# Attention of a macaron block: projections from seven block products, two steps at a time

## The chip, the cores and the metric

The kernel runs on one core of a Trainium2 chip. The metric is the device time of one launch in microseconds. The engines of the core work side by side and synchronise through semaphores: TensorE (in the profile PE for matmuls, PEld for weight loads), VectorE (DVE), ScalarE (ACT), GpSimd (POOL) and SyncE (SP, which here only issues DMAs).

## The reference

A sequence of 2048 tokens with 1024 features passes three parts, each with a residual sum: a feed-forward network (FFN) with weights of plus and minus one, an attention over blocks of 128 tokens behind a convolution of three taps, and the FFN again. All data are f32. Cut to what matters here:

```python
x = x + 0.5 * ffn(layernorm(x))
# attention
c = conv3(layernorm(x), conv_w) + conv_b            # 1024 -> 768 features
q, k, v = split(c, 3)                               # 256 features each, blocks of 128 tokens
qh = einsum('btd,dhe->bthe', q, wq) + bq            # 16 heads of 64
kh = einsum('btd,dhe->bthe', k, wk) + bk
vh = einsum('btd,dhe->bthe', v, wv) + bv
s = einsum('bqhe,bkhe->bhqk', qh / 8, kh)           # causal inside the block
p = softmax(where(causal, s, -1e9))
o = einsum('bhqk,bkhe->bqhe', p, vh)
o = einsum('bqhe,hed->bqd', o, wo) + bo             # 1024 -> 256
x = x + o @ proj_w + proj_b                         # 256 -> 1024
# second FFN
x = x + 0.5 * ffn(layernorm(x))
```

## The kernel before

`P` is 128, `NB` 512, `WC` 2 (256 features in two halves of 128 partitions), `NHP` 8 (16 heads in pairs of two), `NG` 4 groups of 512 tokens with `BPG` 4 blocks each. The kernel runs in order: first FFN, convolution, attention, second FFN. The convolution is done by six transformed tokens at a time. Its outputs leave one word (128 of the 768 features) at a time, first the two words of v, then q, then k (`WORDER`, line 494), each from VectorE (`outputs`, line 613) by SP into a DRAM buffer `qkv_dram`.

The attention's weights `wv_sb`, `wq_sb`, `wk_sb` are loaded during the convolution (line 807), and the first group's words are loaded back as each is stored (`load_qkv`, line 775).

Attention goes through 32 steps, one for each group and head pair (lines 844 and following). Each step has five stages, and a loop (line 1010) starts stage n of step i - n in the order 0, 1, 3, 2, 4:

- `stage_qkv` (846): two matmuls of 512 columns for q and two for k, one for each half of the 256 features, add up in a PSUM bank each; VectorE adds the bias on the way out (892, 894) into the tiles `qk`. At every fourth step (and for the first step both halves at once) the values of four head pairs are computed: for each of four blocks two matmuls of 512 columns, copied out by ScalarE or VectorE (875, 877). The same stage loads the next group's words, the residual rows (`xr`, 857), adds `proj_b` to them on POOL (860), and in group 2 loads the second FFN's weights and takes their signs on ScalarE (853).
- `stage_softmax` (898): for the two heads and four blocks of a step eight score matmuls of 64 rows; ScalarE copies them to SBUF (914), POOL masks (916), VectorE takes the maximum (926), ScalarE the four exponentials of a tile with their sums (929), VectorE normalises (936, 937).
- `stage_transpose` (940): eight transposes on TensorE, one tile copied back by ScalarE (948), one by VectorE (950).
- `stage_values` (953): eight matmuls of 64 output rows, bias by VectorE (967, tile `oT`).
- `stage_wo` (970): two matmuls of 512 columns per step, summed over the eight steps of a group in two banks `acc`; at the end ScalarE adds the bias (985, tile `o2T`).

`stage_proj` (988) follows once for each group: sixteen matmuls of 512 columns, whose banks VectorE adds to the residual rows (1002), which SP stores (1005). Behind the last step, pieces of the second FFN's beginning (`Ffn.fill`, 327: norms, transposes, gate, routing, scaling of its first tiles) are mixed in.

PSUM has four pools of two banks: `mm`, `acc`, `tr`, `sm` (line 72). In `before` q, k, values and output products use `mm`, scores `tr`, transposes and attention outputs `sm`.

A scheduler orders each engine's instructions when the program is built, by priority (program order, unless raised) and by its own estimate of when inputs are there; `pin` (102) keeps an instruction at its place in program order, and inside `tc.manual_schedule` the order written is kept. At run time each engine executes its own list in that order.

## Time and profile before

| what | us |
|---|---|
| median of three runs (968.71 to 968.81) | 968.72 |
| the profiled execution's own time | 967.74 |
| its span, first to last instruction | 965.6 |
| attention: first value product to the second FFN's first main product | 419.0 to 808.9 |
| the last key product to the same end | 766.0 to 808.9 |
| TensorE's granted clock | 0.999 of full speed |

The profile page shows one execution. A line of a group names the line of the kernel, engine, operation, output and inputs, their shape, the count, then the busy time in us and the mean duration of one in ns, and last the idle time of the engine in front of such instructions and what ended it. Matmuls are pipelined: the duration of one overlaps the next, so the time that a matmul costs is read from the distance of starts, or from busy time by count. A line of the order in time has the start, the length, engine, line, operation and count; what stands in brackets is the idle time before it and who ended it.

### The profile page before, as it was taken

The page shows a single profiled execution, that of the slowest core. Times are in us where ns is not written, and L with a number is a line of the kernel's source. Part 1 is how long each engine was busy: PE and PEld are TensorE (multiplying, and loading weights), DVE is VectorE, ACT ScalarE, POOL GpSimd, SP SyncE. Part 2 cuts the span into 40 slices and gives each one's busy share as a digit, 9 for nine tenths or more (in the row PEclk, how much of TensorE's full clock was granted, in tenths as well). Part 3 has the DMA queues.
Part 4 walks back from the last instruction along what each step waited for, and adds up shares of the span by engine and source line. Part 5 has one row for each costly group of instructions (what it writes and reads, how often), then busy time and mean ns, then how long its engine had stood idle before and what let it go on. Part 6 is the DMA issues. An engine that isn't in the chain of part 4 may idle for free.

```text
span 965.6 us, 13859 instructions
## 1 busy us (share of the span) xinstructions
PE 945.2 (98%) x5064; PEld 622.0 (64%) x5064; DVE 639.0 (66%) x1228; ACT 409.2 (42%) x1122; POOL 250.2 (26%) x319
## 2 busy tenths in 40 slices
PE   6999999999999999999999999999999999999997
PEld 4688878876666666655555455545554556878786
DVE  5798887799975566637656455646555665666654
ACT  5586665421111111125546254626452662444441
POOL 2555443410011011003313121212122312434341
PEclk9999999999999999999999999999999999999999
DMA  9776553698497675326030430044004216646331
GB/s 339 171 198 194 160 175 133 233 255 328 164 269 189 181 185 122 96 94 244 12 121 1 139 129 18 1 150 155 2 0 162 57 23 206 180 138 176 109 109 66
DMA packets 37522, 137.21 MB, mean 142 GB/s; under 512 B 4872, under 2 KB 5896, under 8 KB 35536
## 3 DMA queue, kind: packets, MB, share of 16 engines
q1 hardware_dynamic: 28336, 98.69, 28.3%
q0 software_dynamic: 8384, 29.63, 15.9%
q10 hardware_dynamic: 736, 8.02, 2.2%
q8 instruction: 40, 0.66, 0.3%
q14 instruction: 26, 0.21, 0.1%
HBM read 81.70 MB, written 37.85 MB: 124 GB/s over the span
## 4 chain that ended last, share of the span: by engine, by line
PE 54%; issue 30%; POOL 7%; DVE 4%; DMA 3%; ACT 3%; POOLq 0%; DVEq 0%; ACTq 0%
PE cv L542 22%; PE pm_f L309 20%; POOL xr L860 4%; PE tr_f L218 3%; PE pp L994 2%; POOL p L916 2%; DMA x<-in_x_dram 2%; PE lgp_f L226 2%; PE is_f L270 1%; PE tr L429 1%; DVE st_f L166 1%; DMA win<-xw 1%; ACT p L929 1%; PE po_f L293 0%; PE rt_f L258 0%
## 5 line engine op out<-in xcount | busy, mean ns | idle before, releaser
L309 PE MATMUL pm_f<-sw,y_f 128*128 128x512 f32 x1024 | 259.4, 404 | 0.6 <-ACT y_f L283 0.4
L309 PEld LDWEIGHTS pm_f<-sw,y_f 128*128 128x128 f32 x1024 | 187.3, 190 | 42.1 <-ACT y_f L283 0.8
L542 PE MATMUL cv<-v,u 128*128 128x342 f32 x576 | 166.0, 450 | 0.0
L542 PEld LDWEIGHTS cv<-v,u 128*128 128x128 f32 x576 | 109.0, 189 | 56.8
L916 POOL TENSOR_SCALAR_AFFINE_SELECT p<-p 128x512 f32<-128x512 f32 x64 | 39.7, 645 | 277.6 <-ACT p L914 230.1
L929 ACT ACTIVATE p<-p,anm 128x128 f32<-128x128 f32 x256 | 99.0, 389 | 7.1 <-DVE anm L926 7.1
L284 POOL TENSOR_TENSOR y_f<-xnT_f,y_f 128x512 fp32r<-128x512 f32 x63 | 79.8, 1281 | 65.2 <-ACT y_f L283 65.2
L321 DVE TENSOR_TENSOR pm_f<-pm_f,os_f 128x512 f32<-128x512 f32 x64 | 44.6, 697 | 69.4 <-PE pm_f L309 66.7
L559 ACT ACTIVATE m<-cv 128x342 f32<-128x342 f32 x42 | 19.2, 456 | 158.5 <-PE cv L542 157.1
L914 ACT COPY p<-sc 128x512 f32<-128x512 f32 x64 | 34.3, 587 | 104.0 <-PE sc L904 103.9
L926 DVE TENSOR_REDUCE anm<-p 128x4 f32<-128x512 f32 x64 | 40.9, 681 | 47.2 <-POOL p L916 47.2
L975 PE MATMUL acc<-oT,wo_sb 128*128 128x512 f32 x128 | 65.4, 595 | 0.0
L883 PE MATMUL pq<-qkv,wq_sb 128*128 128x512 f32 x128 | 60.6, 593 | 0.0
L883 PE MATMUL pq<-qkv,wk_sb 128*128 128x512 f32 x128 | 60.1, 592 | 0.0
L542 PE MATMUL cv<-v,g 128*128 128x342 f32 (+2 forms) x224 | 57.1, 415 | 0.9 <-DVE v L464 0.9
L994 PE MATMUL pp<-pw_sb,o2T 128*128 128x512 f32 x128 | 57.1, 599 | 0.4 <-DVE xr L1002 0.2
L867 PE MATMUL pv<-wv_sb,qkv 128*128 128x512 f32 x128 | 56.1, 592 | 0.0
L219 ACT COPY xnT_f<-tr_f 128x512 f32<-128x512 f32 x62 | 35.8, 587 | 46.1 <-PE tr_f L218 44.5
L530 DVE SCALAR_TENSOR_TENSOR u<-g,u 128x1024 f32<-128x1024 f32 x18 | 22.0, 1223 | 44.1 <-issue 41.4
L542 PEld LDWEIGHTS cv<-v,g 128*128 128x128 f32 x224 | 39.7, 190 | 17.6 <-DVE v L464 1.3
L929 ACT ACTIVATION_READ_ACCUMULATOR p<-p,anm 128x1 f32 x256 | 48.1, 188 | 0.0
L937 DVE TENSOR_TENSOR p<-p,asum 128x512 f32<-128x512 f32 x64 | 45.6, 712 | 2.2
(138 smaller groups left out, 1469.9 us busy)
## 6 DMA issues: line engine op xcount, KB each, us to landing
g<-in_conv_w_dram SPq DMA_DIRECT2D x28, 512.0 KB, 5.3
u<-in_conv_w_dram POOLq DMA_DIRECT2D x24, 512.0 KB, 6.4
x<-in_x_dram SPq DMA_DIRECT2D x16, 512.0 KB, 4.5
raw<-in_weight_t_dram SPq DMA_DIRECT2D x16, 512.0 KB, 6.6
x<-hbias POOLq DMA_DIRECT2D x16, 512.0 KB, 5.4
x<-x SPq DMA_DIRECT2D x16, 512.0 KB, 4.1
xr<-x SPq DMA_DIRECT2D x16, 512.0 KB, 6.6
x<-xr SPq DMA_DIRECT2D x16, 512.0 KB, 3.9
```

What stands on the lines that cost most here:

```text
L284: lows[h].tensor_tensor(yl, y, yh.bitcast(F32), ALU.subtract)
L309: ins = nc.tensor.matmul(pms[h], lhsT=y[:, n, c, :], rhs=self.sw[:, c, ts(h, NB)], start=(c == 0 and n == 0), stop=(c == DC - 1 and n == 1),)
L321: nc.vector.tensor_tensor(pms[h], pms[h], o, ALU.mult)
L542: nc.tensor.matmul(accs[w, k][:, lo:hi], lhsT=uk[:, c, :], rhs=V[k][:, c, lo:hi], start=(c == 0), stop=(c == DC - 1),)
L867: nc.tensor.matmul(pv, lhsT=qkvs[g][2][:, c, ts(b, P)], rhs=wv_sb[:, c, ts(half, NB)], start=(c == 0), stop=(c == WC - 1),)
L883: nc.tensor.matmul(pq, lhsT=w_sb[:, c, ts(hp, P)], rhs=qkvs[g][n][:, c, :], start=(c == 0), stop=(c == WC - 1),)
L916: nc.gpsimd.affine_select(out=p, in_=p, pattern=[[0, BPG], [-1, P]], compare_op=ALU.is_ge, fill=NEG_INF, base=0, channel_multiplier=1,)
L926: nc.vector.tensor_reduce(nmax, p, AX.X, ALU.max, negate=True)
L929: nc.scalar.activation(p[:, b, :], p[:, b, :], AF.Exp, bias=nmax[:, b : b + 1], accum_out=asum[:, b : b + 1],)
L937: nc.vector.tensor_tensor(p, p, asum.unsqueeze(2).broadcast_to([P, BPG, P]), ALU.mult)
L975: nc.tensor.matmul(accs[g][m], lhsT=wo_sb[:, hp, ts(m, P)], rhs=oT, start=(hp == 0), stop=(hp == NHP - 1),)
L994: nc.tensor.matmul(pp, lhsT=o2T[:, m, ts(b, P)], rhs=pw_sb[:, m, ts(h, NB)], start=(m == 0), stop=(m == WC - 1),)
```

## The change

Queries and keys of two steps (256 weight columns by 512 tokens, 256 features to sum over) are written as a product of two-by-two blocks and computed by seven block products instead of eight, after the scheme of Strassen in Winograd's form: sums of weight blocks (`row_sums`) and of token blocks (`column_sums`) are formed first, and each product's PSUM bank is read between products, so that one bank collects four products and the other three, each read giving one term of the four output blocks. Values are computed the same way, 256 tokens by 1024 weight columns at a time.

- In `seven`, a unit's products 0, 2, 4, 6 go to a bank of `mm` and 1, 3, 5 to one of `tr`; product 3 starts its bank anew, the others add. After each, `Leave` reads the bank: products 0, 2, 3, 6 by ScalarE (which writes the output half with bias and scale), products 1, 4, 5 by VectorE (which adds into it). Two units go in turn: q and k, or two pairs of token blocks for the values. The reads have raised priority.
- A block product of q or k has 256 moving columns, of v 512.
- Weight sums are formed once, on POOL; token sums for each group, for q on POOL, for k on VectorE, for v on POOL.
- The loop goes over 16 pairs of steps with TensorE's order written out: products of pair i, `wo` of pair i - 2, transposes of i - 1, scores of i, attention outputs of i - 1; at the first pair of a group (but the first) then the group's values, at the second pair the output product of the group before. Pieces of the second FFN stand between the stages of the last pairs.
- The four score banks of a pair, two of `mm` and two of `tr`, are copied by ScalarE before any exponential of the pair (`issue_after`).
- `proj_b` is added to the residual rows by an accumulating DMA that POOL issues, instead of a POOL operation. The residual rows are loaded one group later. The ring of rows has 6 buffers instead of 8, and four more are opened for the second FFN. The loads of the q, k and v words and of the FFN weights are placed anew.

```diff
+    def by_rows(w, extra):
+        w4 = w.rearrange("p c (i two e) -> p c i two e", two=2, e=P)
+        e3 = extra.rearrange("p n (i e) -> p n i e", e=P)
+        a11, a12, a21, a22 = (w4[:, j, :, i, :] for i in range(2) for j in range(2))
+        return {"a11": a11, "a12": a12, "s1": a21, "a22": a22, "s2": e3[:, 0], "s3": e3[:, 1], "s4": e3[:, 2]}
+
+    def row_sums(eng, parts):
+        a11, a12, a21, a22, s2, s3, s4 = (parts[n] for n in ("a11", "a12", "s1", "a22", "s2", "s3", "s4"))
+        eng.tensor_tensor(s3, a11, a21, ALU.subtract)
+        eng.tensor_tensor(a21, a21, a22, ALU.add)
+        eng.tensor_tensor(s2, a21, a11, ALU.subtract)
+        eng.tensor_tensor(s4, a12, s2, ALU.subtract)
...
+    def column_sums(eng, parts):
+        b11, b12, b21, b22, t2, t3, t4 = (parts[n] for n in ("b11", "t1", "b21", "b22", "t2", "t3", "t4"))
+        eng.tensor_tensor(t3, b22, b12, ALU.subtract)
+        eng.tensor_tensor(b12, b12, b11, ALU.subtract)
+        eng.tensor_tensor(t2, b22, b12, ALU.subtract)
+        eng.tensor_tensor(t4, b21, t2, ALU.subtract)
+
+    def seven(units):
+        for n, (sums, a, b) in enumerate((
+            (0, "a11", "b11"),
+            (1, "a12", "b21"),
+            (0, "s2", "t2"),
+            (1, "s1", "t1"),
+            (0, "s3", "t3"),
+            (1, "s4", "b22"),
+            (0, "a22", "t4"),
+        )):
+            for name, rows, cols, u, width, leave in units:
+                if n < 2:
+                    leave.sums[n] = bank(("mm", "tr")[n], [P, width], f"{name}_{n}")
+                nc.tensor.matmul(
+                    leave.sums[sums],
+                    lhsT=rows[a][:, u, :],
+                    rhs=cols[b],
+                    start=n in (0, 1, 3),
+                    stop=True,
+                    skip_group_check=True,
+                )
+                with tc.high_priority(offset=400):
+                    leave(n, leave.sums[sums])
+
+    class Leave:
+        def __init__(self, parts, put, more):
+            self.parts, self.put, self.more, self.sums = parts, put, more, {}
+
+        def __call__(self, n, acc):
+            i, first = {0: (0, 1), 1: (0, 0), 2: (1, 1), 3: (3, 1), 4: (3, 0), 5: (1, 0), 6: (2, 1)}[n]
+            (self.put if first else self.more)(self.parts[i], acc, i // 2)
...
-    rring = pool(b3, "rring", 8)
+    rring = pool(b3, "rring", 6)
...
+        tokens_of(0)
+        row_sums(nc.gpsimd, wk_parts)
+        token_sums(0, (nc.gpsimd, nc.vector))
...
+                def put(h, acc, j, n=n):
+                    bias = (sbq, bk_sb)[n][:, 2 * r + j : 2 * r + j + 1]
+                    nc.scalar.activation(h, acc, AF.Identity, bias=bias, scale=(QSCALE, 1.0)[n])
+
+                def more(h, acc, j, n=n):
+                    if n == 0:
+                        nc.vector.scalar_tensor_tensor(h, acc, QSCALE, h, ALU.mult, ALU.add)
+                    else:
+                        nc.vector.tensor_tensor(h, acc, h, ALU.add)
...
-                if n == 0:
-                    nc.vector.tensor_scalar(h, pq, bq_sb[:, hp : hp + 1], QSCALE, ALU.add, ALU.mult)
-                else:
-                    nc.vector.tensor_scalar(h, pq, bk_sb[:, hp : hp + 1], None, ALU.add)
...
+        def load_residual(g):
+            for t in range(g * BPG, (g + 1) * BPG):
+                rows[t] = rring.tile([P, D], F32, name=f"xr_{t}", tag="x")
+                pin(nc.sync.dma_start(out=rows[t], in_=x2[t]))
+                pin(nc.gpsimd.dma_start(out=rows[t], in_=proj_b.broadcast_to([P, D]), accum_op=ALU.add))
...
+        with tc.manual_schedule(engines={mybir.EngineType.PE}):
+            for i in range(LAST + 2):
+                g, r = divmod(i, NP)
+                if i == 0:
+                    stage_v(0)
+                if i < LAST:
+                    if r == 1 and g + 1 < NG:
+                        tokens_of(g + 1)
+                        vxs[g + 1] = values_of(g + 1)
+                    stage_qk(g, r)
+                    if r == NP - 1 and g + 1 < NG:
+                        token_sums(g + 1, (nc.gpsimd, nc.vector))
+                if r == 0 and g > 0:
+                    load_residual(g - 1)
+                for c in range(2):
+                    if i in SIGNS:
+                        signs(SIGNS[i] + c)
+                two(stage_wo, i - 2)
+                if i == LAST:
+                    some(4)
+                two(stage_transpose, i - 1, "sm", "tr")
+                if i < LAST:
+                    stage_scores(g, r)
+                two(stage_values, i - 1)
+                if i < LAST and r == 0 and i > 0:
+                    stage_v(g)
+                if i == LAST - 1:
...
+                    parts = ffn.fill()
+                    some(1)
+                if r == 1 and g > 0:
+                    stage_proj(g - 1)
+            some(len(parts))
```

## The prediction, made before the changed kernel was run

> **What bounds the kernel now.** I read the page's head first, then the busy times of two stretches, the TensorE groups with shapes kept apart, and the order of work over one step of attention.
>
> ```profile
> span 965.6 us, 13859 instructions
> ...
> PE 945.2 (98%) x5064; PEld 622.0 (64%) x5064; DVE 639.0 (66%) x1228; ACT 409.2 (42%) x1122; POOL 250.2 (26%) x319
> ```
>
> TensorE is busy for 98% of the span; no other engine passes 66%. In the stretches (PE, PEld, DVE, ACT, POOL; a count of instructions behind each) the first line is all of attention, the second its end, from the last key product to the first product of the last FFN:
>
> ```profile
> 419.00:808.90 389.90, 387.00 (x2020) 204.80 (x2018) 226.41 (x400) 187.91 (x666) 86.26 (x94) 1.00 0.26 87
> 766.00:808.90 42.90, 40.59 (x272) 22.97 (x271) 22.93 (x44) 21.04 (x61) 9.60 (x12) 1.00 0.39 96
> ```
>
> TensorE idles 2.9 us in attention, 2.3 of them at the end; VectorE stands at 58%, ScalarE at 48%. So TensorE work taken out of attention comes off the time, as long as no new wait appears. What is taken out has these prices:
>
> ```profile
> L542 PE MATMUL cv<-v,u 128*128 128x342 f32 x576 | 166.0, 450 | 0.0
> ...
> L883 PE MATMUL pq<-qkv,wq_sb 128*128 128x512 f32 x128 | 60.6, 593 | 0.0
> L883 PE MATMUL pq<-qkv,wk_sb 128*128 128x512 f32 x128 | 60.1, 592 | 0.0
> ...
> L867 PE MATMUL pv<-wv_sb,qkv 128*128 128x512 f32 x128 | 56.1, 592 | 0.0
> ...
> L542 PE MATMUL cv<-v,g 128*128 128x256 f32 x32 | 7.2, 378 | 0.0
> ```
>
> The count shows that an f32 matmul of the program is two instructions on the chip (q: 32 steps x 2 blocks = 64 matmuls, 128 instructions). "Mean" holds the pipeline's tail; the pace is what counts. The order of work in a step:
>
> ```profile
> 651.22 1.88 PE L883 MATMUL pq<-qkv,wq_sb 128*128 128x512 f32 x4
> 652.94 1.88 PE L883 MATMUL pq<-qkv,wk_sb 128*128 128x512 f32 x4
> ...
> 653.14 0.75 DVE L892 TENSOR_SCALAR qk<-pq,bq_sb 128x512 f32<-128x512 f32 x1 [1.89 <-PE pq L883]
> ...
> 660.68 0.40 ACT L929 ACTIVATE p<-p,anm 128x128 f32<-128x128 f32 x1
> ...
> 661.07 0.40 ACT L929 ACTIVATE p<-p,anm 128x128 f32<-128x128 f32 x1
> ...
> 779.99 1.04 ACT L219 COPY xnT_f<-tr_f 128x512 f32<-128x512 f32 x2
> ...
> 780.60 0.43 PE L226 MATMUL lgp_f<-xnT_f,gate_sb 128*32 128x128 f32 x8 [1.83 <-ACT xnT_f L219]
> ```
>
> Four q instructions take 652.94 - 651.22 = 1.72 us, 0.43 each. VectorE reads 0.20 us after the last one's pace ends (653.14). Exponentials follow one another every 0.39 us. TensorE starts about 0.03 us after the ScalarE result it needs (first of the two copies, 779.99 + 0.58).
>
> **The change, part by part.**
>
> *Products.* At 342 columns an instruction paces at 166.0/576 = 0.288 us. At 256 columns 32 took 7.2 us in two runs, each with one tail of 378 - 216 ns, so (7.2 - 0.32)/32 = 0.215; 0.288 x 256/342 gives 0.216 too. Queries and keys of two steps: before, 16 instructions x 0.43 = 6.88 us; after, 2 x 7 products x 2 instructions x 0.216 = 6.05. Gain 0.83 x 16 pairs = 13.3 us. Values: 128 x 0.43 = 55.0 becomes 112 x 0.43 = 48.2, gain 6.9. Together **-20.2 us**.
>
> The row of 256 columns (0.215 us) says that the narrower product is paced by its columns alone. The Trainium skill, TensorE: Matmul & The Clock Gate, "Why this matters for your kernels", speaks against narrowing: at least 85% of peak only with all dimensions at 512 or more. If that made 256 columns cost 0.216/0.85 = 0.254 us (an estimate from that page), q and k would lose 28 x 0.254 - 6.88 = 0.23 us a pair instead of gaining 0.83, 17 us worse in all, and the kernel would be slower. I go by the row: it is the same type, height and engine.
>
> *Waits between products.* Product n+2 of a unit adds into the bank that product n's reader must have left. With q and k in turn that is 4 x 0.43 = 1.72 us from start to start. The way round: product 0.43, wake 0.15 to 0.20 (a ScalarE copy of a value bank starts at 420.97, its four instructions at 419.10), read, 0.03 back. The ScalarE read (256 wide, bias by pointer) is not in the trace; o2T, the same form at 512, takes 676 ns, and copies of 128 and 512 columns 253 and 587, 0.87 ns a column, so 0.676 - 0.22 = 0.46. VectorE: 512 columns 0.69, 342 columns 0.52, so 0.43. The round is 1.07 to 1.10 us. The wait sits on the weight load, which starts some 0.2 us ahead of its matmul, so about 0.42 us is spare. An exponential under way holds ScalarE for at most 0.39, within it; a VectorE operation (reduce 0.68, oT 0.74) for up to 0.75, 0.3 over, in the two VectorE reads of a unit that a product waits for (the second and the fifth). Load of an ordinary pair without value or output work, 15.5 us of TensorE (6.05 + wo 3.44 + transposes 1.8 + scores 2.2 + values 2.1): ScalarE 4 copies 2.1, 16 exponentials 6.2, two pT copies 1.2, eight reads 3.0 = 12.5 (81%); VectorE reduces 2.6, reciprocals and products 3.5, oT 1.5, pT 1.4, six reads 2.6 = 11.6 (75%). The eight ScalarE reads are new there; the four VectorE bias adds of 0.75 go. Bounds for the stall of a pair: 0, and 1.54 us (one tile's four exponentials ahead of a read). I take 0.25, near the lower end since the usual hold fits the spare time: **+4 us** over 16 pairs.
>
> *Values into queries.* The first k product needs the bank of the second value unit, read by a copy of 0.58 us that starts 0.15 after the last value product, while q's first product covers 0.43: 0.3 us, four times: **+1.4 us** with the restart. Within the value products two units of 0.86 us give 3.4 us a round against 0.86 + 0.15 + 0.58 or 0.70: no stall. VectorE's 24 and ScalarE's 32 reads there lie under 12 us of TensorE.
>
> *Softmax of two steps together.* In nine rounds no value or output work follows the scores; the transposes come 2.1 + 6.05 + 3.44 = 11.6 us after the last score (the fourth tile's 1.3 later). ScalarE frees at +1.2 (two copies, 1.07), then 16 exponentials x 0.39 = 6.2 and six reads of the next pair 2.2 bring +9.6, reciprocal and product 0.9 more: 10.5 against 12.9. Nothing, with 2.4 us spare; if a wait ahead of the exponentials eats that, the transposes stall and with them everything behind in TensorE's written order.
>
> *Head of attention.* v of the first group is loaded long before. The store of the last k half is issued at 424.6 and its reload goes out at 428.45; today keys are first needed at 434.5, in the new order at 431.1 + 1.3 (419.05 + 12.0 of value products). Landing takes 2.6 to 4.7 us, so 431.1 to 433.2; then three VectorE sums (256 wide, 0.43) before the first t2 product at 433.2. Bounds 0 and 4; **+1.5 us**. On POOL the key weight sums (4 x 1.28, the row of 128x512 tensor operations) stand ahead of the query sums (4 x 0.65): 7.7 us from 424.6, done by 432.3. The query and value weight sums, 8 x 1.28 = 10.2 us, fall in the convolution, where POOL only issues DMAs with 2 to 8 us idle before each; SP holds the weight loads up to 10 us, which the taps, a word ahead, cover: 0, or up to 2 if not.
>
> *End of attention.* The last softmax now has four tiles: 10.5 - 2.2 (no reads) = 8.3 us, plus three normalisations of 1.24 and two copies of 0.58 on ScalarE = 13.2. Before it TensorE has values 2.1, wo 3.44 and some 3.4 of FFN pieces, whose own chains wait in the written order. That leaves 4.3 idle; then o2T before the output product about 1, and the first scaling, now behind the output product instead of ahead of it, about 1: 6.3 against the 2.3 idle today: **+4 us**, bounds 0 and 9.
>
> *The rest.* The POOL adds of proj_b (16 x 2.36 = 38 us) become accumulating DMAs (16 x 0.90 on POOL, 5.4 to land): neither is on the path, since the output product comes a whole round later; in the last group 12 us remain against 6.6 + 5.4, so 0, at most 2. Sums for later groups lie on POOL and VectorE in a round's last 9 us. Loads, stores and sign loads move within SP, whose DMA share is 0.26. SP blocked by a ring of six costs nothing while rows are read a round ahead.
>
> Sum: -20.2 + 4 + 1.4 + 1.5 + 4 = **-9.3 us**. The profiled execution took 967.74 (span 965.6 and 2.1 around it), so 958.4; the median of the runs shown, 968.72, lies 1.0 above it, which gives **959.4**.
>
> **Rivals.**
> - *Slower: the ScalarE queue.* It runs in written order. One tile's exponentials that still wait for their reduce stand ahead of a read: 4 x 0.39 = 1.54 us a pair, 24.6 instead of 4, so 980. It decides from 13.3/16 = 0.83 us a pair. For it: ScalarE at 81%, and 7.1 us idle before exponentials for that reason today. Against: reads are marked urgent, and all reduces end within about 4 us of the last score. The trace shows ScalarE starts only in order; the Trainium skill, same page, "Architectural detail", calls ScalarE and VectorE strict FIFO, which is what lets this rival live but gives no price.
> - *Softmax and end late.* 0.4 us in each of nine rounds and 6 at the end: 959.4 + 3.6 + 2 = 965. For it: 2.4 us spare only.
> - *All covered.* Only the 1.4 at the values stays: 968.7 - 20.2 + 1.4 = 950. For it: TensorE never waits today.
> - *No gain at 256 columns.* A 128-column weight load paces the product. L309 at 512 columns runs 16 in 3.86 us, 0.241 each: q and k gain 6.88 - 28 x 0.241 = 0.13 a pair, 2 instead of 13.3, so 970.6. Against: the 256-column row.
>
> **How the numbers follow.** Forecast 0.45 (955 to 964); late softmax 0.15; all covered 0.10; ScalarE queue 0.25 (972 to 988); weight loads 0.05. Faster by over 0.2% (2 us, about what a measurement of this kernel can tell from no change) is the first three, 0.70; within it 0.05; slower 0.25. The range leaves out the upper half of the queue's case and little below: 950 to 978; the likeliest case alone 955 to 964.
>
> **What would show it.** Right: products of 256 columns every 0.216 us; 8 and 6 reads a pair of about 0.46 and 0.43; idle time ahead of the q and k products below 0.4 us a pair; TensorE about 367 us busy in attention. Wrong: idle before these products put down to ScalarE reads (queue), idle before transposes (softmax), or a pace near 0.24.

## The result, and the profile after

The changed kernel takes 971.3 us (median of 20 runs) where the kernel before, on the same chip, takes 968.7 (20 runs). The ratio is 1.003 with an interval of 1.002 to 1.004: slightly slower. The forecast was 959.4, faster. The profiled execution of the changed kernel took 970.66; its span is 968.8, against 965.6 before, so 3.2 us have to be explained, and 9.3 us of gain that did not come.

The head of the page:

```profile
span 968.8 us, 14538 instructions
...
PE 930.2 (96%) x5240; PEld 662.9 (68%) x5240; DVE 649.8 (67%) x1289; ACT 464.6 (48%) x1262; POOL 268.4 (28%) x363
```

TensorE has 15.0 us less to do (945.2 to 930.2), yet idles 38.6 us instead of 20.4. The busy times of the same two stretches as before (all of attention; its end from the last key product to the first product of the second FFN):

```profile
421.76:806.09 384.33, 367.63 (x2169) 245.37 (x2167) 228.85 (x452) 240.57 (x800) 84.90 (x122) 0.98 0.39 115
756.49:806.09 49.60, 43.17 (x257) 24.67 (x255) 25.21 (x52) 22.18 (x67) 11.81 (x18) 0.93 0.86 237
```

TensorE is busy 367.6 us in attention, as forecast (about 367), though partly by luck: 11.3 us that the new order of work saves (below) were not in the forecast. It waits there 16.7 us instead of 2.9, 6.4 of them at the end, and its clock, 1.00 before, is down to 0.93 at the end. The groups of the new products and their reads:

```profile
L826 PE MATMUL pq<-x,wq_sb 128*128 128x256 f32 x96 | 31.2, 407 | 0.9 <-DMA x<-qkv 0.5 <-DVE qk L953 0.4
L949 ACT ACTIVATE qk<-pq,sbq 128x256 f32<-128x256 f32 x64 | 30.0, 469 | 45.8 <-PE pq L826 45.7
L955 DVE TENSOR_TENSOR qk<-pq,qk 128x256 f32<-128x256 f32 x48 | 20.2, 422 | 0.3
L826 PE MATMUL pq<-t,wq_sb 128*128 128x256 f32 x32 | 9.5, 379 | 0.0
```

The reads last 0.47 and 0.42 us (0.46 and 0.43 were assumed). The last line has the mean of a product without a wait, 379 ns, as the 378 of the convolution's 256 columns. So the products are not the surprise. The waits are, and they sit in few places. In the order of work at the head of attention (start, length, idle time before and who ended it):

```profile
434.42 0.67 PE L826 MATMUL pq<-x,wq_sb 128*128 128x256 f32 x2 [0.48 <-DMA x<-qkv]
436.07 0.67 PE L826 MATMUL pq<-x,wk_sb 128*128 128x256 f32 x2 [0.98 <-ACT qk L949]
...
438.92 0.67 PE L826 MATMUL pq<-x,wk_sb 128*128 128x256 f32 x2 [1.75 <-DMA x<-qkv]
...
441.06 1.19 PE L826 MATMUL pq<-t,wk_sums 128*128 128x256 f32 x2 [1.04 <-DVE t L809]
442.04 1.06 PE L826 MATMUL pq<-x,wq_sb 128*128 128x256 f32 x2
442.90 1.06 PE L826 MATMUL pq<-x,wk_sb 128*128 128x256 f32 x2
...
457.31 0.63 PE L1031 MATMUL pt<-ident,p 128*128 128x128 f32 x4 [0.58 <-DVE p L1024]
459.39 0.63 PE L1031 MATMUL pt<-ident,p 128*128 128x128 f32 x4 [1.46 <-DVE p L1024]
```

The first pair's queries and keys take 12.4 us (434.4 to 446.8) instead of 6.05: TensorE waits for keys on their way back from DRAM, then for VectorE's token sums, then runs at half pace (442.04 to 442.90: two instructions in 0.86 us instead of 0.43). The keys' second half is late because its reload stands behind the store of its own word. SP's issues in order of time (SPq), and its own wait:

```profile
428.49 0.32 SPq L640 DMA_DIRECT2D qkv<-y  x1
...
433.37 0.32 SPq L783 DMA_DIRECT2D x<-qkv  x1
```

```profile
SPq L783 <- DMA qkv<-y: 2.0, 1, 2.0
```

The first three halves go out at 428.9, 429.4 and 430.3, right behind the store of the last word; the fourth waits until that store has landed (4.9 us after its issue) and itself lands 5.4 us after its own, at 438.8. The first key half lands at 435.98, so the wait that ends at 436.07 is most likely for it, although the profile puts it down to a ScalarE read.

Pair 0's transposes wait for the softmax. ScalarE's order in time shows why it is long. The first and the last of pair 0's sixteen exponentials, with one of the reads of pair 1's products that stand among them:

```profile
450.85 0.44 ACT L1016 ACTIVATE p<-p,anm 128x128 f32<-128x128 f32 x1
...
451.67 0.47 ACT L949 ACTIVATE qk<-pq,sbq 128x256 f32<-128x256 f32 x1
...
459.36 0.40 ACT L1016 ACTIVATE p<-p,anm 128x128 f32<-128x128 f32 x1
```

They take 8.9 us; in the kernel with eight products everywhere (below), where VectorE reads q and k, 6.2:

```profile
444.26 0.40 ACT L996 ACTIVATE p<-p,anm 128x128 f32<-128x128 f32 x1
...
450.05 0.39 ACT L996 ACTIVATE p<-p,anm 128x128 f32<-128x128 f32 x1
```

The longest wait of the end, from the list of TensorE's waits:

```profile
PE acc L1061 <- DVE oT L1053: 4.2, 1, 4.2
```

and what stands ahead of that `oT` in VectorE's queue (its order in time):

```profile
764.13 1.27 DVE L166 BATCH_NORM_STATS2 st_f<-xf 128x6 f32<-128x512 f32 x2
...
766.20 1.87 DVE L1012 TENSOR_REDUCE anm<-p 128x4 f32<-128x512 f32 x3 [0.54 <-POOL p L1002]
768.48 0.69 DVE L1012 TENSOR_REDUCE anm<-p 128x4 f32<-128x512 f32 x1 [0.41 <-POOL p L1002]
...
769.17 0.72 DVE L1053 TENSOR_SCALAR oT<-ao,bv_sb 128x512 f32<-128x512 f32 x1
```

The attention outputs of pair 14 end at 765.7; their bias on VectorE comes at 769.17, behind the FFN's norm sums and the last softmax's four maxima, two of which wait for POOL.

For the experiments the span is cut at four points of TensorE's order: first value product, first output weight product of group 0 (`acc`), end of the last key product, first main product of the second FFN. The pieces are called head, middle, end, and behind. Within the changed order of work each stretch holds the same work in every kernel, unless the text says otherwise (the row of before holds it mixed differently: its end has about 2.1 us less of work):

| kernel | first value product at | head | middle | end | behind | span |
|---|---|---|---|---|---|---|
| before | 419.1 | 40.6 | 306.5 | 42.8 | 156.7 | 965.6 |
| changed | 421.8 | 51.8 | 283.0 | 49.6 | 162.7 | 968.8 |
| eight products everywhere | 420.3 | 43.1 | 294.3 | 52.4 | 160.5 | 970.7 |

Each row is one profiled execution. In the profiles of kernels whose head is written like the changed one's it lies between 49.1 and 53.3 us.

### The profile page after: what moved, and what is told of

It is laid out like the page before. It is cut to its first block, busy times and chain, and to the rows that moved or that the text cites. A ratio compares the mean times of both kernels' runs of the same rounds, so it can differ in the third digit from the quotient of the medians.

```text
span 968.8 us, 14538 instructions
## 1 busy us (share of the span) xinstructions
PE 930.2 (96%) x5240; PEld 662.9 (68%) x5240; DVE 649.8 (67%) x1289; ACT 464.6 (48%) x1262; POOL 268.4 (28%) x363
## 4 chain that ended last, share of the span: by engine, by line
PE 45%; ACT 4%; DVE 2%; issue 1%; POOL 1%; POOLq 0%; ACTq 0%; DVEq 0%
PE pm_f L309 12%; PE pq L826 7%; PE pp L1086 6%; PE acc L1061 5%; PE pv L826 4%; PE sc L989 3%; PE ao L1044 2%; PE pt L1031 2%; ACT p L1016 1%; PE tr_f L218 1%; PE lgp_f L226 1%; PE is_f L270 1%; ACT qk L949 1%; ACT p L998 0%; DVE t L807 0%
## 5 line engine op out<-in xcount | busy, mean ns | idle before, releaser
L309 PE MATMUL pm_f<-sw,y_f 128*128 128x512 f32 x1024 | 262.8, 407 | 0.7 <-ACT y_f L283 0.4
L1061 PE MATMUL acc<-oT,wo_sb 128*128 128x512 f32 x128 | 60.3, 616 | 4.2 <-DVE oT L1053 4.2
L949 ACT ACTIVATE qk<-pq,sbq 128x256 f32<-128x256 f32 x64 | 30.0, 469 | 45.8 <-PE pq L826 45.7
L1036 DVE COPY pT<-pt 128x512 f32<-128x512 f32 x32 | 22.1, 690 | 39.0 <-PE pt L1031 39.0
L295 ACT ACTIVATE os_f<-po_f 128x512 f32<-128x512 f32 x64 | 34.7, 595 | 28.1 <-PE is_f L270 17.9
L1061 PEld LDWEIGHTS acc<-oT,wo_sb 128*128 128x128 f32 x128 | 25.1, 198 | 30.0 <-issue 24.6
```

Of the source, the lines that this page charges most:

```text
L309: ins = nc.tensor.matmul(pms[h], lhsT=y[:, n, c, :], rhs=self.sw[:, c, ts(h, NB)], start=(c == 0 and n == 0), stop=(c == DC - 1 and n == 1),)
L949: nc.scalar.activation(h, acc, AF.Identity, bias=bias, scale=(QSCALE, 1.0)[n])
L1061: nc.tensor.matmul(accs[g][m], lhsT=wo_sb[:, hp, ts(m, P)], rhs=oT, start=(hp == 0), stop=(hp == NHP - 1),)
```

## The experiments

Each edit is cut to what matters; where a kernel builds on another one of this list, the edit is shown against that one. Each ratio is to the kernel before on the same chip.

### Four runs that split the loss

**The value sums moved on POOL.** The first group's value sums are pinned behind the last tap load of the convolution; nothing but POOL's order changes.

```diff
-        row_sums(nc.gpsimd, parts)
+        row_sums(nc.gpsimd, parts, pin if g == 0 else lambda ins: ins)
```

> The changed kernel with one edit: the four POOL sums over the first group's value words are queued behind the last tap DMA of the convolution; the order of every other engine stays. Theory (POOL's queue): in the changed kernel these sums wait 11.0 and 10.2 us on POOL for the value words to land, and the accumulating tap DMAs queued behind them go out 4 and 6 us later than before, which is what makes TensorE wait 2.8 us for u in the convolution. Expected: no wait of cv for u, the first value product some 3 us earlier (about 418.5 instead of 421.8), time about 968 against 971. Rival (the POOL weight sums slow VectorE through shared memory ports, so u is late anyway): cv still waits, time 971.

Measured: 968.4 us, ratio to before 1.000 (0.999 to 1.001); the first value product starts at 418.9 instead of 421.8, and TensorE no longer waits for taps in the convolution, as expected. In the changed kernel POOL's order in time is

```profile
301.55 0.72 POOL L795 TENSOR_TENSOR vs<-vx 128x256 f32<-128x256 f32 x1 [11.02 <-DMA vx<-qkv]
302.23 0.87 POOL L520 DMA_DIRECT2D u<-in_conv_w_dram  x1
...
329.70 0.72 POOL L796 TENSOR_TENSOR vx<-vx 128x256 f32<-128x256 f32 x1 [10.21 <-DMA vx<-qkv]
...
331.96 0.88 POOL L520 DMA_DIRECT2D u<-in_conv_w_dram  x1
```

and with the sums moved

```profile
294.58 0.87 POOL L520 DMA_DIRECT2D u<-in_conv_w_dram  x1 [3.66 <-DMA u<-in_conv_w_dram]
...
325.50 0.87 POOL L520 DMA_DIRECT2D u<-in_conv_w_dram  x1 [6.94 <-DMA u<-in_conv_w_dram]
```

A sum that waits 11 us for its operand holds the tap loads queued behind it; they go out 6 to 8 us later than with the sums moved, and TensorE then waits 2.8 us for taps. So 3 us of the loss are a queue position in the convolution, a place that the change does not seem to touch.

**Eight products.** The new order of stages with plain eight products of 512 columns, no sums.

```diff
-            seven(units)
+            for c in range(WC):
+                nc.tensor.matmul(pq, lhsT=w_sb[:, c, ts(hp, P)], rhs=xs[g][:, c, :], ...)
```

> The changed kernel with the old eight products in the new order: q, k and v by the plain two-block matmuls of 512 columns, biases on VectorE, no sums of weights or tokens; everything else (pairs, written order, DMAs of proj_b, the end) stays. Theory: the products cost 20.2 us more, but the waits between products (6 us), the waits of the first pair for sums (7 us) and the convolution's wait (3 us) go, and the pairs' order keeps its 0.6 us a pair: about 971 + 20 - 6 - 7 - 3 = 975, range 971 to 978, above the changed kernel. Rival (the waits between products ate the whole gain of 20 us): without them the time falls to 955 to 963.

Measured: 971.5 us, ratio 1.004 (1.003 to 1.006). The new order with all else that was moved along with it (loads, residual rows, signs) costs about 4 us against before, and the seven products bring about 1 us on top of it (1.9 by the two spans), which the intervals of the two ratios don't tell from nothing. By the table they win 11.3 us in the middle, and lose 8.7 at the head, 1.4 ahead of it and 2.2 behind; 2.8 more lie at the end, where these kernels have the same products, and their cause stays open. The number stands at the lower edge of the theory's; that the waits between products eat their gain is out. The order is not worse everywhere: what a pair does besides its queries and keys takes 9.16 us (3.43 + 1.84 + 1.99 + 1.90 for output weights, transposes, scores, attention outputs) in both new kernels, and 9.78 in two steps of before (8.33 from step to step, less 3.44 of products). Scores and attention outputs of one step of before, and of a pair in the changed kernel:

```profile
654.75 1.16 PE L904 MATMUL sc<-qk,qk 64*128 64x128 f32 x16
655.84 1.09 PE L958 MATMUL ao<-pT,vh 128*64 128x128 f32 x16
```

```profile
478.80 2.06 PE L989 MATMUL sc<-qk,qk 64*128 64x128 f32 x32
480.79 1.97 PE L1044 MATMUL ao<-pT,vh 128*64 128x128 f32 x32
```

From start to start 16 scores take 1.09 us, 32 of them 1.99. With fewer changes from one kind of matmul to another TensorE gains 0.6 us a pair, 9.8 in all, which the forecast did not have. The loss is ahead of attention and at its two ends.

**A filled array.** Matmuls into an unused bank stand where TensorE waits in pair 0 and ahead of the output weights of pair 14, to see whether the fallen clock costs the time.

```diff
+                if i == LAST:
+                    fill_array("mm", 10, wo_sb[:, 0, 0:P], wo_sb[:, 0, 0:HT])
                 two(stage_wo, i - 2)
```

> The changed kernel with useless matmuls of 256 columns (their results are read by nobody) in three places where TensorE waits: 9 in the first pair's products, 10 ahead of the last but one pair's output sums. Theory (granted clock): the waits there let the granted clock fall, and the products behind run at twice their duration (0.85 instead of 0.43 us; 6.1 instead of 3.4 us for the eight output-sum instructions at the end). With the array kept busy the clock stays at 1.00 there and 3 to 5 us come off: 966 to 968. Rival (the waits alone set the time, the low clock is hidden in them): 970 to 973, whatever the clock shows.

Measured: 972.3 us, ratio 1.005 (1.003 to 1.006), in the rival's range. At the end the filler takes 4.4 us in the place of the wait, and the output weights behind it run in 3.43 us instead of 6.1; but TensorE waits longer behind them, and the end shrinks only from 49.6 to 48.5. So half pace follows from the waits and costs some 2.7 us at the end, and with filler most of that is waited for elsewhere. For the head the run settles nothing: pair 0 takes 11.0 us instead of 12.4, but pair 1 waits 2.9 us for a VectorE read behind maxima whose masks stand, in this kernel, behind three value sums on POOL, and the head grows from 51.8 to 54.6.

**`oT` first.** The bias of the attention outputs gets raised priority on VectorE.

```diff
-            nc.vector.tensor_scalar(oT, po, ...)
+            with tc.high_priority(offset=400):
+                nc.vector.tensor_scalar(oT, po, ...)
```

> The changed kernel with raised priority for the VectorE bias that ends the attention outputs (oT). Theory: at the end of attention oT stands in VectorE's queue behind the reduces of the last softmax, and these wait for POOL; TensorE waits 4.2 us for it, its clock falls, and the next matmuls run at half pace. Expected: that wait goes, but the last softmax still ends at about 774 and the FFN's pieces wait for ScalarE behind its exponentials, so only 1 to 3 us come off: 968 to 970. Rival (oT is the only cause of the late end): 963 to 965.

Measured: 971.8 us, ratio 1.005 (1.003 to 1.006), above the 968 to 970 expected. TensorE waits 2.5 instead of 4.2 us for `oT`, and 1.5 for the FFN's `xnT` instead of 0.2; the end is 48.2 instead of 49.6. A single wait removed is followed by the next one: what is missing there is work for TensorE.

### Work for the end, and three tries at the head

**The output product in two halves.** Group 2's output product, 13.8 us, does blocks 0 and 1 at its old place and blocks 2 and 3 behind the attention outputs of pair 14.

```diff
                 if r == 1 and g > 0:
-                    stage_proj(g - 1)
+                    stage_proj(g - 1, range(2) if g == NG - 1 else range(BPG))
+                if i == LAST - 1:
+                    stage_proj(NG - 2, range(2, BPG))
```

> The output product of group 2 is done in two halves: two blocks at its place (second pair of the last group), two blocks, 6.9 us, behind the attention outputs of pair 14, ahead of the output weights of pair 14. Nothing is left out. Theory: at the end TensorE has nothing to do while it waits for oT (4.2 us), then runs 2.7 us longer at a lower clock, and waits again for the last softmax and norms; 6.9 us of products that need none of these lie in their place. The stretch from the last key product to the second FFN's first main product becomes about as long as it is now (49.6) with 6.9 us moved into it, so the time falls by 4 to 7 us to 964 to 967. Rival: the FFN pieces' own chains over VectorE, ScalarE and POOL set the end, and these run no earlier: the stretch grows by 5 to 7 us and the time stays at 969.5 to 972.

Measured: 966.9 us, ratio 0.998 (0.997 to 1.000). The end is 52.1 with 7.0 us of work moved into it. The wait for `oT` is gone; what remains in TensorE's waits of that stretch is led by

```profile
PE is_f L270 <- DVE xr L1094: 2.5, 1, 2.5
```

VectorE's last residual sums were late: it waited 7.2 us for a residual row, and these rows were loaded only behind the moved product. The theory holds, and the 2.5 us name the next step (the rows, below).

**Keys without their reload.** The first group's second key half is loaded from a word stored long before, that of the first key half (word 2 in the edit; the expectation names the queries). This kernel leaves out the reload of the last word, and the first group's keys are therefore other numbers.

```diff
+            w = 2 if (n, c, g) == (1, 1, 0) else n * WC + c
-            nc.sync.dma_start(out=dst[:, c, :], in_=qkv_dram[n * WC + c][:, ts(g, NB)])
+            nc.sync.dma_start(out=dst[:, c, :], in_=qkv_dram[w][:, ts(g, NB)])
```

> In this kernel the second half of the first group's keys is loaded from the word that holds the first half of its queries, which was stored long before, so the wait for the store and reload of the convolution's last word is gone; the first group's keys are therefore other numbers. Theory: this wait, and the three VectorE sums behind it, hold the key products of the first pair, which took 12.38 us for queries and keys together instead of 6.05. The loads still go out only at about 428.9 us, because their tiles come free then, land some 4.5 us later, and the sums end at about 435; so the first pair takes 6.1 to 7.5 us, and the time falls by about 5 us, from 971.3 to 966 (964 to 968). Rival: the wait only moves, since the transposes of the first pair wait for its softmax anyway: 970 to 972, with the wait of pair 1's transposes longer than today's 3.9 us by what was gained.

Measured: 969.1 us, ratio 1.001 (1.000 to 1.002), between theory and rival. Pair 0 takes 9.9 us instead of 12.4, not 6.1 to 7.5. Of the 2.2 us gained not all need come from it: kernels with the same head as the changed one (the moved value sums, the early rows below) have 9.8 and 13.9 us there. The keys still wait 0.40 us for their loads and 1.44 for the token sums:

```profile
437.93 0.67 PE L827 MATMUL pq<-x,wk_sb 128*128 128x256 f32 x2 [0.40 <-DMA x<-qkv]
440.46 0.67 PE L827 MATMUL pq<-t,wk_sums 128*128 128x256 f32 x2 [1.44 <-DVE t L810]
```

The wait for the store's landing is only a part of the loss: without it the fourth load goes out at 431.7 instead of 433.4 and lands 6.1 us later. The four loads are late as a group, since in SP's queue they stand behind the last store, which goes out only when VectorE has finished the last word (428.8 here). Whether their tiles would have been free earlier no run shows.

**Another order at the head.** Queries of pairs 0 and 1, then keys of both, both scores, then pair 2's queries and keys, then the first transposes.

```diff
+                    if i == 0:
+                        for n in range(2):
+                            seven([stage_qk(0, m, (n,), False)[0] for m in range(2)])
+                    elif i == 1:
+                        stage_scores(g, r)
+                        stage_qk(0, 2)
```

> TensorE's written order at the head of attention is another one: after the first group's values the queries of pairs 0 and 1, then the keys of pairs 0 and 1, the scores of 0, the scores of 1, queries and keys of pair 2, and only then the transposes of pair 0; the outputs and probabilities of these pairs lie in buffers of the row ring, which is empty then. Nothing is left out. Theory: the head costs about 13 us (keys wanted before they are reloaded, 6.3; transposes of pair 0 without cover from an output product, 3.9; scores 1.3; the rest in pair 1's products), and this order gives the keys 6 us more and the softmax 8 instead of 6 us. From the end of the value products to the start of the products that follow pair 0's attention outputs is 32.6 us today for 19.8 of work; with pair 2's products in it 25.9 of work and 2 to 5 of waits. The time falls by 8 to 10 us to 961 to 964. Rival: the reload ends late whatever the order, or the softmax of pair 0 needs over 12 us: gain under 4, 967 to 972.

Measured: 973.2 us, ratio 1.004 (1.003 to 1.006): refuted. The head is 50.0 instead of 51.8, and the convolution's end is later (425.7), TensorE waiting 4.6 us there for taps instead of 2.8. A new wait, in the kernel with this order and the moved value sums:

```profile
455.95 1.22 PE L826 MATMUL pq<-x,wq_sb 128*128 128x256 f32 x2 [5.61 <-ACT p L1010]
```

Pair 2's products need the banks of pair 1's scores, whose copies stand in ScalarE's queue behind pair 0's sixteen exponentials.

**Three moves together**: the value sums moved, the new order at the head, the output product in halves.

> The changed kernel with three moves together: the first group's value sums stand behind the last tap loads on POOL, the new order at the head, and the output product of group 2 in two halves. If the three causes are the right ones and independent, the gains add: 971.3 - 3.2 - 9 - 5.5 = 953.6 (950 to 958), below the kernel before. Rival: the gains lie beside each other, because VectorE's or ScalarE's total work sets the pace once TensorE's waits are gone: 960 to 966.

Measured: 964.5 us, ratio 0.996 (0.995 to 0.998). The rival's range: the head gave nothing, and the other two add up as measured one by one (2.9 and 4.4 off 971.3 make 964.0).

**Copies first.** The value sums moved and the new order at the head, with both pairs' scores copied ahead of any exponential, and POOL forming the query token sums ahead of the key weight sums.

```diff
-                        stage_scores(g, r)
+                        stage_scores(0, 0, (1,))
...
-        row_sums(nc.gpsimd, wk_parts)
         token_sums(0, (nc.gpsimd, nc.vector))
+        row_sums(nc.gpsimd, wk_parts)
```

> The value sums of the first group behind the last tap loads, and the new order at the head, with two more moves: the scores of pairs 0 and 1 are copied by ScalarE before any exponential of pair 0, and POOL forms the first group's query token sums ahead of the key weight sums. Nothing is left out. Theory: the new order alone brought nothing because the copies of pair 1's scores stood in ScalarE's queue behind the 16 exponentials of pair 0, so that the banks for pair 2's products came free 5.6 us late, and because the query sums stood behind 5.4 us of key weight sums on POOL (1.0 us). With both gone, the stretch from the first value product to the first output weight product, 51.7 us in the changed kernel and 50.0 with the new order alone, comes to 45 to 47, and the time to 964 to 967. Rival: the exponentials only start later by the copies' 2.1 us and the transposes of pair 0 wait in place of the products: stretch 49 to 50, time 967 to 969.

Measured: 972.6 us, ratio 1.004 (1.003 to 1.006), head 51.7: refuted, worse than its rival. The 5.6 us are gone; instead the transposes wait for ScalarE's exponentials and the attention outputs for a copy that now stands behind pair 1's exponentials:

```profile
467.02 3.68 PE L1056 MATMUL ao<-pT,vh 128*64 128x128 f32 x32 [4.25 <-ACT pT L1046]
```

**Rows early.** The value sums moved, the output product in halves, and the last group's residual rows loaded ahead of its second half.

```diff
+                    load_residual(NG - 1)
                     stage_proj(NG - 2, range(2, BPG))
```

> The value sums of the first group behind the last tap loads, the output product of group 2 in two halves, and the residual rows of the last group loaded ahead of its second half instead of behind it. Nothing is left out. Theory: in the kernel with the output product in two halves VectorE waited 7.2 us for the residual rows (loaded late, the accumulating DMA lands 9 us after its issue), so that its last sum kept a bank 2.5 us from the second FFN's first scaling; loaded 10 us earlier they are there. 971.3 - 3.2 (conv) - 4.5 (two halves) - 2.5 = 961 (959.5 to 963). Rival: scaling of the second FFN's first tile is held by its own chain, and only the convolution's and the halves' gains stay: 963 to 965.

Measured: 962.6 us, ratio 0.994 (0.993 to 0.996). The end is 49.5 with 7.0 of work moved in, 42.5 without; the wait of 2.5 is 0.5. As the theory has it.

**Signs apart.** The second FFN's weight rows are loaded one or two pairs ahead of their signs.

> The rows of the second FFN's weights are loaded one or two pairs ahead of their signs: four rows at pairs 6 and 10, signs two at a time at pairs 7, 8, 11, 12. Nothing is left out. Theory: a sign whose row has not landed holds ScalarE's queue, and with it the reads of q and k and the copies of the scores; in pairs 6 and 7 TensorE loses 0.6 and 1.7 us to that, so the time falls by 2 to 3 us to 968.5 to 969.5. Rival: ScalarE's own work, 1.06 us for each sign in pairs where it is 80% busy, is what costs, and it is only moved: 970.5 to 972.

Measured: 973.6 us, ratio 1.005 (1.004 to 1.007), above both ranges. Pair 6 still has 2.70 us for its scores and pair 7 7.83 for its products (2.56 and 7.74 in the changed kernel). This run tells nothing: the scheduler put the signs as early as before, the rows were loaded from 558.8 on, and ScalarE's waits between 540 and 590 us are the old ones:

```profile
ACT sw L1106 <- DMA raw<-in_weight_t_dram: 4.7, 4, 2.1
```

The question is taken up again in the last run.

**All moves together**: value sums moved, copies first, halves, early rows, signs apart.

> All moves together: value sums behind the tap loads, the new order at the head with copies first and query sums first, the output product of group 2 in two halves with the last residual rows loaded ahead, and the signs apart from their loads. Nothing is left out. If the waits are the causes and independent, 965.5 - 4.5 - 2.5 - 2.5 = 956 (953 to 959). Rival: the gains lie beside each other, 960 to 964.

Measured: 964.7 us, ratio 0.997 (0.995 to 0.998), just above the rival's range. The end is 49.5 as with the early rows alone, the head 53.3: reordering stages brought the head nothing.

### What the head is made of

**Eight products for the first two pairs.** Only the first group's values and the queries and keys of pairs 0 and 1 go back to eight products; their sums follow behind.

```diff
-                    stage_qk(g, r)
+                    (plain_qk if i < 2 else stage_qk)(g, r)
+                    if i == 1:
+                        token_sums(0, (nc.gpsimd, nc.vector))
...
+                if i == 2:
+                    column_sums(nc.gpsimd, wv_parts)
+                    for parts_ in (wq_parts, wk_parts):
+                        row_sums(nc.gpsimd, units_of(parts_, 0, 2))
```

> Only the first group's values and the queries and keys of pairs 0 and 1 are plain eight products of 512 columns again, read once; the sums of tokens and of the weight columns that these pairs use are formed behind them, the value weight sums too, and the next group's tokens are loaded a pair later. All else is the changed kernel. Nothing is left out. Theory: the head's 51.7 us from the first value product to the first output weight product are long because its seven products wait for sums formed late and for reads that stand in line, not because of the order of the stages: the stretch comes to about 43, as in the kernel with eight products everywhere, though 3.4 us of products are added; and since the value sums are gone from POOL's queue in the convolution, the first value product stands at about 419 to 420. Time 971.3 - 8.7 - 2.5 = 960 (958 to 962.5). Rival: the order does it (no output product between the first pairs to cover the softmax, keys wanted before their reload): stretch 48 to 52, time 966 to 970.

Measured: 964.9 us, ratio 0.997 (0.996 to 0.998), between theory and rival. The products no longer wait (6.96 us for pair 0), but the head is 49.1, not 43, because pair 0's transposes take 7.7 us instead of 2.6. VectorE's order in time there:

```profile
446.77 1.24 DVE L1053 TENSOR_TENSOR p<-p,asum 128x512 f32<-128x512 f32 x1
...
448.79 1.04 DVE L1053 TENSOR_TENSOR p<-p,asum 128x512 f32<-128x512 f32 x1
```

and the same operations with eight products everywhere:

```profile
446.79 0.69 DVE L1004 TENSOR_TENSOR p<-p,asum 128x512 f32<-128x512 f32 x1
...
448.26 0.69 DVE L1004 TENSOR_TENSOR p<-p,asum 128x512 f32<-128x512 f32 x1
```

In the first POOL forms sums from 445.2 to 455.3, in the second it has none there. A further part is the masks, two of which stand behind a value sum each in POOL's queue; the first of these sums (442.7) waits 0.8 us for its operand.

**The same head with the better end** (halves and early rows).

> The same head, with the output product of group 2 in two halves and the last residual rows loaded ahead. Nothing is left out. Theory: the gains at both ends of attention are independent: 960 - 5.8 = 954 (952 to 957), the 5.8 being what halves and rows brought on top of the moved value sums (968.4 to 962.6). Rival: 958 to 962, if the head's gain is not there.

Measured: 957.9 us, ratio 0.989 (0.988 to 0.991): the gains add (964.9 less the 5.8 makes 959.1). It is the rival's lower edge, since the head had given less than the theory wanted (it is 51.2 in this profile).

**Eight products for the whole first group.** No sum of its tokens, the weight sums on POOL in pieces behind the masks of pairs 2 to 4, the next group's token sums behind those of pair 2.

```diff
-                    (plain_qk if i < 2 else stage_qk)(g, r)
+                    (plain_qk if g == 0 else stage_qk)(g, r)
...
+                if i in (2, 4):
+                    with tc.issue_after(masked[i]):
+                        for parts_ in (wq_parts, wk_parts):
+                            row_sums(nc.gpsimd, units_of(parts_, i - 2, i))
```

> The whole first group (values, queries, keys of pairs 0 to 3) by plain eight products, no sums of its tokens, and the weight sums on POOL in pieces behind the selects of pairs 2 to 4; the next group's token sums all on POOL behind the selects of pair 2; the end as with halves and early rows. Nothing is left out. Theory: in the kernel with eight products for pairs 0 and 1 alone the transposes of pair 0 waited 4.6 us because POOL's sums ran beside and between the first softmax's operations (VectorE's 512-column products took 1.04 to 1.24 us there instead of 0.69, selects stood behind sums); with no sum near the first softmax the stretch from the first value product to the first output weight product falls from 49.0 to 43 to 44.5, as in the kernel with eight products everywhere, and the time from 957.9 to 953 (951 to 955), 0.8 us of more products counted. Rival: the sums cost as much where they now lie, beside the softmax of pairs 2 to 4: 956 to 959, with transposes of pairs 2 to 4 longer than 2 us.

Measured: 953.6 us, ratio 0.986 (0.984 to 0.987), the theory's number. The head is 43.2:

```profile
441.02 3.70 PE L972 MATMUL pq<-x,wq_sb 128*128 128x512 f32 x8
444.56 3.60 PE L972 MATMUL pq<-x,wk_sb 128*128 128x512 f32 x8
448.00 1.47 PE L1060 MATMUL pt<-ident,p 128*128 128x128 f32 x12
450.04 0.63 PE L1060 MATMUL pt<-ident,p 128*128 128x128 f32 x4 [0.57 <-DVE p L1053]
```

One wait of 0.57 us in the first transposes, where the changed kernel had waits of 0.58, 1.46 and 0.92 behind a pair 0 twice as long. So the head's loss comes with the seven products and not from the order of the stages: their sums are late ahead of the first products, and their sums or reads fall into the first softmax, the reads on ScalarE in the changed kernel, the sums on POOL in the one with eight products for two pairs. This kernel takes away both sums and reads; no run leaves the sums where they were and takes away the reads alone.

**The better end without any seven products.**

```diff
-            seven(units)
+            for c in range(WC):
+                nc.tensor.matmul(pq, lhsT=w_sb[:, c, ts(hp, P)], rhs=xs[g][:, c, :], ...)
...
+                    load_residual(NG - 1)
+                    stage_proj(NG - 2, range(2, BPG))
```

> Plain eight products everywhere, no sums at all, in the new order, with the output product of group 2 in two halves and the last residual rows loaded early: the last kernel (953.6) without its seven products in groups 1 to 3. Nothing is left out. Theory: there the seven products bring what the phases show, 6.97 - 6.5 us for queries and keys in each of twelve pairs and 13.84 - 12.15 for the values of three groups, 5.5 + 5 = 10.5 us: 964 (962 to 966). Rival: their reads and sums cost elsewhere what they save, and the moved work at the ends did it all: 954 to 959.

Measured: 966.9 us, ratio 0.999 (0.998 to 1.000), just above the theory's range and 13.3 us above the kernel before it in this list. In the middle, where the products of groups 1 to 3 lie, it is 11.1 us, as the phases had given (10.5); 5 more lie at the end, where both have the same products, and stay open. So the seven products do pay, where nothing waits for their sums.

**Signs behind the copies.** To the kernel with the first group by eight products and the better end: weight rows loaded at pairs 6 and 10, two signs each held behind the score copies of the pair before.

```diff
+                        with tc.issue_after(copies[i - 1]):
                             signs(SIGNS[i] + c)
```

> The kernel with the first group by eight products and the better end; besides, the rows of the second FFN's weights are loaded at pairs 6 and 10 and each two signs are held behind the score copies of the pair before theirs (pairs 6, 7, 10, 11), so that they can no longer stand early in ScalarE's queue. In the first try the signs had been placed by the scheduler as early as before, and ScalarE still waited 4.7 us for rows. Nothing is left out. Theory: the wait of signs for their rows costs TensorE 0.5 us in pair 6's scores (2.49 instead of 1.99) and 1.0 to 1.5 in pair 7's products (7.52 instead of 6.05 to 6.46); both go, and the time falls from 953.6 by 1.5 to 2, to 952 (950.5 to 953). Rival: the signs' own 1.06 us each are what costs, wherever they stand in the full queue: 953 to 955, with TensorE's loss in pair 7 or 8 instead.

Measured: 950.8 us, ratio 0.982 (0.981 to 0.984). Pair 6's scores take 1.98 us and pair 7's products 6.46, as in any other pair, and ScalarE waits for no row. So the late rows had cost it: 4.1 us of ScalarE's waits and, by the middle of the two profiles, some 1.6 of TensorE's time. It is the fastest kernel here, 18 us below the kernel before:

```profile
span 948.6 us, 14375 instructions
...
PE 925.8 (98%) x5196; PEld 652.5 (69%) x5196; DVE 644.1 (68%) x1271; ACT 450.4 (47%) x1226; POOL 267.2 (28%) x367
```

TensorE is again busy for 98% of the span, as in the kernel before, with 19.4 us less to do. The stretches of the last kernels:

| kernel | first value product at | head | middle | end | behind | span |
|---|---|---|---|---|---|---|
| value sums moved | 418.9 | 49.1 | 284.1 | 49.6 | 162.3 | 964.1 |
| halves and early rows | 419.4 | 53.3 | 277.4 | 49.5 | 162.0 | 961.6 |
| first group by eight, better end | 418.3 | 43.2 | 276.6 | 49.5 | 162.0 | 949.6 |
| eight everywhere, better end | 418.8 | 43.1 | 287.7 | 54.6 | 160.9 | 965.1 |
| first group by eight, better end, signs behind | 418.9 | 43.1 | 275.0 | 49.5 | 162.1 | 948.6 |

(In the kernels with the better end 7.0 us of work have moved from the middle to the end.)

## Why the prediction was wrong

By the terms of its sum, against the span's 3.2 us. A phase is a run of TensorE instructions of one kind; "measured" counts its length above its length without waits.

| term | forecast | measured |
|---|---|---|
| seven products for eight | -20.2 | -20.2 |
| waits between products, values into queries | +5.4 | +6.3 |
| softmax of two steps, middle | 0 | +1.8 |
| order of stages by pairs | not seen | -9.8 |
| output products of groups 0 to 2 | not seen | -1.5 |
| head of attention | +1.5 | +13.4 |
| POOL's sums in the convolution | 0, at most 2 | +2.7 |
| end, with the second FFN's start | +4 | +10.7 |
| sum | -9.3 | +3.4 |

*Right.* The price of the products: 6.05 us for a pair (28 instructions of 0.216 us) and 12.1 for a group's values. The convolution's row of 256 columns held, and the estimate of 0.254 us for a narrow product, weighed in the prediction, did not.

*Right in size, partly by luck: the waits between products.* Over pairs 2 to 15 a pair takes 6.46 or 6.55 as a rule, 6.05 behind an output product, 7.74 once. So an ordinary pair waits 0.4 us where 0.25 was taken, the first pair behind a group's values only 0.1 more, where 0.3 was taken, and 1.3 of the sum are the one pair whose reads stand behind a late sign. The rival of the ScalarE queue did not come (1.54 us a pair was its price, 0.4 is the rule), nor the weight loads' pace. That 971.3 lies beside these two rivals' numbers (972 and up, 970.6) is chance.

*Wrong: the head, the term that decided.* Two steps of its working failed. The first is the reload of the last key half, out at 428.45 and landed by "431.1 to 433.2". Its times were taken from the old kernel. In the changed one the store of that word goes out at 428.49 instead of 424.6 (the convolution ends 2.7 us later, and two value reads of VectorE, 1.2 us, stand between the last operations of the word), the reload at 433.37 once the store has landed, and its landing takes 5.4 us instead of "2.6 to 4.7"; TensorE waits for the half until 438.9 and for its sums until 441.1. With the half pace behind, pair 0's products cost 6.3 us more than without waits. The second step is the softmax's cover, "11.6 us" behind the last score, taken for pair 0 as for any other. Pair 0 is followed by neither attention outputs nor output weights, only by pair 1's products, 6.9 us (449.2 to 456.1), while its softmax ends 11.6 us behind the last score (460.8), 1.1 later than the working has it, with eight reads of the next pair in ScalarE's queue instead of six. Its transposes cost 3.9 us more, the scores behind them 1.3. What the runs put in the place of both: with the seven products, their sums and their reads taken away from the first group, the 8.7 us against the kernel of eight products are back (43.2 and 43.1).

*Wrong: the end.* Its bounds were 0 and 9. The stretch costs 4.7 (49.6 - 42.8 less the 2.1 of mixed work), near the forecast by luck: the 4.2 us of waiting for `oT` and the 2.7 of half pace behind it are not in its working, and the 4.3 of idle time ahead of the last transposes did not come. Then the second FFN starts with less prepared: from its first main product to the end it takes 162.7 us instead of 156.7, and 5.0 of these 6.0 are lost over its first 32 main products (14.9 us instead of 9.9). The prediction counted the scaling behind the output product as "about 1". No run here brought these 6.0 us back: all kernels in the new order have 160.5 to 163.3. What would is open.

*Wrong: "the taps, a word ahead, cover".* The cost of POOL's sums was looked for in their own 10.2 us and in SP; it came from two sums of the values, not of the weights, that wait in POOL's queue for their operands.

*Wrong in the other direction:* 9.8 us for TensorE's longer runs of one kind of matmul. Without them the change would have cost some 12 us instead of 2.6. The prediction counted work and waits and took the lengths of transposes, scores and outputs as fixed.

## What to carry to other kernels

When products are saved by sums, cost the sums and the reads by their place in each queue, most of all at the first use, where no earlier work covers them: here the first group by plain products and the sums later was worth more than any reordering. A wait that has lost its cover is mended with work for the waiting engine (half an output product moved to the end, 4.4 us), not with priority or filler (1.4 and 1.1 us of the end, and no shorter time). And an instruction that waits for its data in an in-order queue holds every DMA queued behind it, also in a stage that the change does not touch.

## What the runs showed of the hardware

VectorE's products of two tensors last 1.04 to 1.24 us for 512 columns while POOL forms sums of 256 columns (eight products for the first two pairs), and 0.69 without; POOL's own sums go there from 0.72 to as much as 1.18. The Trainium skill, SBUF — State Buffer, "SBUF: two separate sides", says that VectorE operations with two SBUF inputs and GpSimd operations lock a shared pair of ports for a whole instruction. The direction agrees; one POOL sum ahead of each product would make 0.69 + 0.72 = 1.41 (an estimate from these rows and that rule), and the longest seen is 1.24. A sum already under way would leave less, so these rows do not tell whether the lock is whole.

The clock falls without a long gap. Within 434.4 to 441.1 us of the changed kernel TensorE's longest idle time between products was 1.75 us (the others 0.48, 0.98 and 1.04), and the products that follow have half pace. The granted clock stands third from the end:

```profile
440.00:444.30 4.30, 3.26 (x9) 2.69 (x9) 1.30 (x4) 1.73 (x4) 0.00 (x0) 0.60 1.03 402
```

It is 0.60. The Trainium skill, TensorE: Matmul & The Clock Gate, "Why this matters for your kernels", asks for no idle gap above about 3 us; here gaps of at most 1.75 us in 7 us were enough. With gaps of 0.59, 0.94, 0.40 and 1.44 at the same place the keys without their reload kept 1.00 (434 to 444 us), so the two cases lie close together; whether the longest gap or the sum of them decides, no run separates.

Runs of one kind of matmul pay: the same matmuls of a pair took 9.16 us in four phases and 9.78 in the finer mixture, as said above. An accumulating DMA of 512 KB needed 9.3 us from issue to landing (median of 16), where the forecast had taken 5.4 from another transfer; in the kernel with the output product in halves, where the rows come late, VectorE waited 7.2 us for one of them, and TensorE then 2.5 for VectorE.
